# A gated two-layer network with attention and experts on one core: biases of the second attention, order of its statistics, fillers of the search, and scatters of list halves

## Chip, cores and metric

The kernel runs on one core of one Trainium2 chip. The metric is the time of one launch on the device, in microseconds (us). Before the change it is 1257.83 us, the median of three runs (1257.43 to 1258.2).

The engines are named as in the profile: PE is TensorE (PEld its weight loads), DVE is VectorE, ACT is ScalarE, POOL is GpSimd, SP is SyncE, which here only issues DMAs.

## What is computed

`x` holds 8 batches of 256 tokens with 256 features, `ctx` the same shape. Everything is float32. Two layers follow each other, each of an attention and a feed-forward part with experts:

```python
x = x + tanh(g_xattn[0]) * attention0(layernorm(x), ctx, ctx)     # 16 heads of 16, causal mask
x = x + tanh(g_ffn[0])   * ffn0(layernorm(x))                     # 8 experts, each token goes to 2
x = x + tanh(g_xattn[1]) * attention1(layernorm(x), ctx, mask)    # 16 heads of 16, mask on keys
x = x + tanh(g_ffn[1])   * ffn1(layernorm(x))                     # 16 experts + a shared one
```

In `ffn1` it is the experts who choose: a softmax over 16 experts gives scores, and each expert takes the 256 tokens with the highest score (of 2048):

```python
scores = softmax(flat_x @ gate_w.T).T               # 16 x 2048
topk_weight, topk_idx = top_k(scores, 256)
h  = gelu(flat_x[topk_idx] @ Wg[e].T) * (flat_x[topk_idx] @ Wu[e].T)
eo = (h @ Wd[e].T) * topk_weight[..., None]
out = zeros.at[topk_idx].add(eo) + (gelu(x @ Sg.T) * (x @ Su.T)) @ Sd.T     # the last term: the shared expert
```

## The kernel before

A scheduler orders the instructions of DVE, ACT, POOL and SP. PE's order is that of the program text wherever the text stands in `manual_schedule`, and every engine works through its instructions in order. All 2048 tokens lie in SBUF as 16 tiles of 128 tokens (`x`); a batch is two tiles.

**Stages.** First attention (about 0 to 340 us), the routing of the first FFN (337 to 358), its 8 experts (358 to 538, 22.45 us each), then the remaining projections of keys and values for the second attention (`Kv1`, 538 to 551.9), the second attention (551.9 to about 813), the choice of tokens for the 16 experts (813 to 897), the 16 experts (897 to 1247, 22.24 us each) and the last scatter (to 1258.5).

**First FFN** (`ffn0`, L745). An expert transposes its gathered rows (`rtr`, L765), multiplies (`b` L775, `a` L777, `yps` L785) and adds its results to the rows of a table in memory through a scatter of GpSimd (`Router.add`, L646; the four scatters of one expert do not wait for each other, but for those of the expert before). At its end it finds the tokens of the expert after the next (`find_tokens`, a one-hot matrix `hot` and a product `idp`).

**Second attention** (`attention1`, L805). Its first lines load weights and biases and work out, for every batch, whether any key is valid (`some`), the query's bias (`bqs`) and the output's bias with the values' bias folded in (`gb`, for which PE multiplies `bv_wide` by `wo` into `gb_ps`, L847). Then come 32 units, `u = 4 b + ch`: batch `b`, and four heads `ch`. For each unit `find_maxima` multiplies queries and keys (`sc`, L901) and takes the maximum for each query (`maxima`, L906, four instructions on DVE); `weigh` multiplies again with the maximum folded in (`scT`, L933) and takes the exponential on ACT (`pT`, L940); `values_of` multiplies by the values (`o_ps`, L949). Every second unit `place_maxima` transposes the maxima (`mtr`, L922) and adds them to the queries (`qT`, L924); `normalise` divides (`on` L962, `o` L970), `put_back` transposes (`otr`, L982), and once a batch `project_out` multiplies by `wo` (`y`, L990) and adds to `x` (L994). `Net.attend` (L137) writes down in which order PE takes these.

Inside `find_maxima` the next batch is prepared: with `ch == 0` the statistics of its layer norm (`norm_stats`, L88), with `ch == 1` its normalisation and transposition (`norm_pair`, L112: `xn` on DVE, L116, and `ln_ps` on PE, L121), with `ch` 2 and 3 the two halves of its query projection (`qproj`, L877; bias and mask on DVE, L889, and ACT, L885). `norm_stats` is 16 instructions for a batch: two `bn_stats` (L94), two `bn_aggr` (L95) and twelve on 128 x 2 elements (L100 to L107) that take a reciprocal square root, each working on the result of the one before. Once a batch is done with attention, `Last.stats` and `Last.norm` do the same for the last layer norm (`xn3`), and `Last.score` its router's softmax.

**Choice of tokens** (`Last.choose`, L1142). The 256th highest score of each expert is found by a search over 30 bits: on DVE a count (`hit`, L1175), on PE its sum (`total`, L1183), on DVE the decision (`drop` L1185, `cand` L1190), and the next bit. So that PE has work meanwhile, the shared expert is a Python generator (`share`, L1099) of 96 steps, and `fill(n)` puts its next `n` steps into PE's order. A step is two records of 128 x 512 or four of 128 x 256 in the trace. It is called with `1 + bit % 2` in each bit (L1195), and with 2, 2, 4 and the rest around the list making: `prefix` (L154) numbers the chosen tokens, DVE turns this into `marks` and `q16`, and `find_tokens(e)` (L1245) makes `hot` (L1252), `idp` (L1258) and `ids` (L1264), with which GpSimd gathers the rows (L1269).

**Experts** (`Last.experts`, L1274). An expert takes 256 tokens as two halves of 128 (`rtr` L1297, `g` and `u` L1310, `act` L1315, `hT` L1316, `ey` L1320, `eo` L1325); each half is added to `out` by a scatter of GpSimd (L1328). The scheduler sees two scatters that read and write `out`, and so lets each wait for the one before.

Of the kernel before, what the change touches and what calls it, by code (L numbers as in the profile page):

```python
# [41 lines left out]
class Net:  # L42
# [92 lines left out]
    def attend(self, n, find_maxima, place_maxima, weigh, values_of, normalise, put_back, extra):  # L135

        with self.tc.manual_schedule(engines={mybir.EngineType.PE}):  # L137
            for s in range(n + 6):
                g = (s - 2) // 2
                if s < n:  # L140
                    find_maxima(s)
                if 0 <= s - 4 < n:
                    values_of(s - 4)
                if s % 2 == 0 and 0 <= g < n // 2:
                    place_maxima(g)
                if s % 2 == 1 and 0 <= g - 2 < n // 2:
                    put_back(g - 2)
                if 0 <= s - 3 < n:
                    weigh(s - 3)
                if s % 2 == 0 and 0 <= g - 2 < n // 2:  # L150
                    normalise(g - 2)
                extra(s)

    def prefix(self, psum, mask, n, tag="a", last=True):  # L154
# [288 lines left out]
class Router:  # L443
# [54 lines left out]
    def take_x(self):  # L498
        for b in range(B):
            t = slice(2 * b, 2 * b + 2)  # L500
            self.after_puts(self.net.nc.sync.dma_start(self.net.x[:, t, :], self.sum_rows[:, t, :]))

    def after_puts(self, dma):
        for name in self.puts:
            self.net.tc.add_manual_dep(
                dma.ins, name,
                mybir.DependencyInfo(mybir.DependencyClass.Sync, mybir.DependencyReason.DATA),
            )

# [136 lines left out]
    def add(self, e, ids, ys):  # L646


        tc = self.net.tc
        done = []  # L650
        for i, y in enumerate(ys):
# [4 lines left out]
            )  # L656
            group = f"sums{e}"
            tc.declare_no_dep(put.ins, group=group, reason="other rows")
            tc.add_to_no_dep_group(group, put.ins)
            self.after_puts(put)  # L660
            done.append(put.ins.name)
# [82 lines left out]

def ffn0(net, w, router, work, nexts, kv1):  # L745

    tc, nc = net.tc, net.nc
    with ExitStack() as es:
# [4 lines left out]
        for e in range(E0):  # L753
# [48 lines left out]
def attention1(net, w, tanh_g, kT, v, router, last, ps_s):  # L802

# [5 lines left out]
    with ExitStack() as es:  # L809
# [6 lines left out]
        wq = one.tile([P, 2, 4, P], F32, name="wq1")  # L816
        wo = one.tile([P, 2, D], F32, name="wo1")
        bq = one.tile([P, 4], F32, name="bq1")
        gb = one.tile([P, D], F32, name="gb1")
        nc.sync.dma_start(wq, w["wq1"])  # L820
        nc.sync.dma_start(bq, w["bq1"])
        nc.sync.dma_start(wo, w["wo1"])
        nc.sync.dma_start(gb, w["bo1"].partition_broadcast(P))

        mask8 = one.tile([P, N], U8, name="mask8b")
        row16 = one.tile([P, 1], F32, name="row16")
        nc.sync.dma_start(mask8, w["mask"].rearrange("a b -> (a b)").partition_broadcast(P))
        nc.sync.dma_start(row16, w["row16"])
        some = one.tile([P, B], F32, name="some")
        rows = one.tile([P, B], F32, name="some_rows")  # L830
        bqs = one.tile([P, B, 4], F32, name="bqs")
        nc.vector.tensor_reduce(some, mask8.rearrange("p (b k) -> p b k", b=B), AX.X, ALU.min)
        nc.vector.tensor_scalar(some, some, -1.0, 1.0, ALU.mult, ALU.add)
        nc.vector.tensor_scalar(rows, some, row16, None, ALU.max)
        nc.vector.tensor_tensor(
            bqs, bq.unsqueeze(1).to_broadcast([P, B, 4]),
            rows.unsqueeze(2).to_broadcast([P, B, 4]), ALU.mult,
        )

        bv = one.tile([P, 2], F32, name="bv1")  # L840
        wide = one.tile([P, 2, P], F32, name="bv1_wide")
        nc.sync.dma_start(bv, w["bv1"])
        nc.vector.tensor_copy(wide, bv.unsqueeze(2).to_broadcast([P, 2, P]))
        ps = ps_s.tile([P, D], F32, name="gb_ps", tag="s")
        with tc.manual_schedule(engines={mybir.EngineType.PE}):
            for kc in range(2):
                nc.tensor.matmul(ps, wide[:, kc, :], wo[:, kc, :], start=kc == 0, stop=kc == 1)  # L847
        nc.vector.tensor_tensor(gb, gb, ps, ALU.add)
        nc.vector.tensor_scalar(gb, gb, tanh_g, None, ALU.mult)

# [42 lines left out]
        def find_maxima(u):  # L893
# [11 lines left out]
            for r in range(4):  # L905
                nc.vector.tensor_reduce(  # L906
                    m[:, u % 2, :, 32 * r + HD + 1], sc[r], AX.X, ALU.max, negate=True
                )
# [119 lines left out]
class Last:  # L1028
# [3 lines left out]
    def __init__(self, net, w, dram, one, few, xnT, tanh_g, out):  # L1032
# [24 lines left out]
        self.shared = None  # L1057

    def stats(self, b):
        self.st = self.net.norm_stats(self.few, (2 * b, 2 * b + 1), 2)  # L1060
# [38 lines left out]
    def share(self, psum):  # L1099
# [3 lines left out]
        for blk in range(N // 512):  # L1103
# [16 lines left out]
            for i in range(4):  # L1120
                t = 4 * blk + i
                y = psum.tile([P, D], F32, name="sy", tag="s")
                for f in range(FS // P):
# [4 lines left out]
                    if f == 3:  # L1128
# [3 lines left out]
                        )  # L1132
                        nc.sync.dma_start(out[:, t, :], o)
                    if f % 2:
# [6 lines left out]
    def choose(self, one, psum):  # L1141

        self.list = one
        with self.net.tc.manual_schedule(engines={mybir.EngineType.PE}):
            self.find_places(one, psum)
            self.fill(2)
            self.nexts = [self.find_tokens(0, psum, "s")]
            self.fill(4)
            self.nexts.append(self.find_tokens(1, psum, "s"))
            self.fill(96)  # L1150

    def find_places(self, one, psum):
# [27 lines left out]
        for bit in range(29, -1, -1):  # L1180
# [39 lines left out]
        )  # L1220
        self.fill(2)
        nc.vector.scalar_tensor_tensor(
# [52 lines left out]
    def experts(self):  # L1275
        net, w, out = self.net, self.w, self.out
        tc, nc = net.tc, net.nc
        with ExitStack() as es:
# [7 lines left out]
            for e in range(E1):  # L1286
# [16 lines left out]
                for f2 in range(F1 // P // 2):  # L1303
# [11 lines left out]
                    nc.scalar.activation(act, g, AF.Gelu)  # L1315
                    nc.vector.tensor_tensor(hT[:, 2 * f2 : 2 * f2 + 2, :], act, u, ALU.mult)  # L1316
                for r in range(2):
                    y = ps_y.tile([P, D], F32, name="ey", tag="y")
                    for f in range(F1 // P):
# [7 lines left out]
                    )  # L1327
                    nc.gpsimd.indirect_dma_start(  # L1328
                        out=out[:, :],
                        out_offset=bass.IndirectOffsetOnAxis(ap=ids[:, r : r + 1], axis=0),  # L1330
                        in_=o, in_offset=None, compute_op=ALU.add,
                    )
                if e + 2 < E1:
                    self.nexts.append(self.find_tokens(e + 2, ps_a, "a"))
# [3 lines left out]
def network(ctx, tc, w, out):  # L1338
# [11 lines left out]
    with ExitStack() as right, ExitStack() as left:  # L1350
# [11 lines left out]
        with ExitStack() as psum:  # L1362
            ps_s = pool(psum, "a0_ps_s", 7, space=PSUM)
            kv1 = Kv1(net, ctxT, w, k1, v1, ctxs, ps_s)
            attention0(net, ctxT, w, tanh_g[:, 0, 0:1], router, kept, ps_s, kv1)
            one, work = pool(left, "f0_one"), pool(left, "f0_work", 2)
            nexts = router.place(one, work, kv1, ps_s)
        ffn0(net, w, router, work, nexts, kv1)
    one, few = pool(ctx, "f1_one", side="right"), pool(ctx, "f1_few", 2, side="right")
    last = Last(net, w, dram, one, few, k1[0], tanh_g[:, 1, 1:2], out)  # L1370
    with ExitStack() as psum:
        ps_s = pool(psum, "a1_ps_s", 7, space=PSUM)
        attention1(net, w, tanh_g[:, 0, 1:2], k1, v1, router, last, ps_s)
        values.close()
# [85 lines left out]
```

## Time and profile before

| what | value |
|---|---|
| median of three runs | 1257.83 us (1257.43 to 1258.2) |
| the profiled execution | 1260.25 us, span 1258.5 us |
| mean granted TensorE clock | 0.979 |
| PE busy | 1198.6 us, 95% of the span |
| PEld / DVE / ACT / POOL busy | 846.0 / 581.9 / 320.9 / 268.7 us |
| PE idle, second attention's first 48 us | 8.1 us, clock 0.75 there |
| PE idle, search (813 to 861) | 2.8 us |
| PE idle, list making (861 to 897) | 4.9 us, clock 0.95 there |

PE is the engine that sets the time, and a busy share of 95% leaves 59.9 us idle in all. The granted clock says more than the busy time does: the same instruction takes twice as long at 0.5, and is counted as busy for all of it. Of the timeline's columns the first is the start in us, the second the time from the first to the last instruction of a group, then engine, line, operation, the tiles (out<-in), shape and how many; in brackets stands the engine's idle time before it and what ended it. Records that follow closely are put into one row, so a row can hold short idle times.

### The profile page before, as it was taken

To read this page: it belongs to the slowest core of one execution; us is meant where nothing else is said; L and a number is where in the kernel's file an instruction comes from. 1 tells how busy PE (TensorE), PEld (TensorE's weight loads), DVE (VectorE), ACT (ScalarE), POOL (GpSimd) and SP (SyncE) were. 2 spreads that over 40 slices of the span, in tenths; PEclk is the share of its full clock that TensorE was granted. 3 is DMA by queue.
4 is the path that set the end of the run, shared out by engine and by line. 5 is a ranking of instruction groups with operands and counts; after the bars stand their busy time and mean duration, and the time that the engine had idled before them with its cause. 6 is when DMAs were issued, how large, how long until landed. Compare 5 with 4: busy or idle time off the path is not lost.

```text
span 1258.5 us, 21894 instructions
## 1 busy us (share of the span) xinstructions
PE 1198.6 (95%) x9145; PEld 846.0 (67%) x9145; DVE 581.9 (46%) x1485; ACT 320.9 (25%) x629; POOL 268.7 (21%) x329
## 2 busy tenths in 40 slices
PE   5899999999999999988999999998999999999997
PEld 5556667777546565555666665644788888888886
DVE  5634656554524332267766675567332232322221
ACT  2333344344221111122444445210101111110110
POOL 1200222232036455230000000000122232322211
PEclk9899999999999999987999999999999999999999
DMA  7000101001425456140000000420165554646531
GB/s 232 2 2 11 60 2 35 18 19 35 137 65 118 106 125 155 27 134 1 1 6 14 11 10 10 161 100 17 54 196 148 184 167 151 191 131 189 165 109 17
DMA packets 49665, 104.31 MB, mean 83 GB/s; under 512 B 7834, under 2 KB 35742, under 8 KB 43294
## 3 DMA queue, kind: packets, MB, share of 16 engines
q1 hardware_dynamic: 37278, 85.73, 19.8%
q0 software_dynamic: 12288, 17.18, 8.2%
q8 instruction: 72, 1.18, 0.4%
q14 instruction: 27, 0.22, 0.0%
HBM read 85.39 MB, written 17.50 MB: 82 GB/s over the span
## 4 chain that ended last, share of the span: by engine, by line
PE 89%; DVE 6%; ACT 1%; DMA 1%; issue 1%; SPq 0%; POOLq 0%; POOL 0%; DVEq 0%; ACTq 0%
PE g L1310 9%; PE u L1310 9%; PE ey L1320 9%; PE proj L237 6%; PE b L775 5%; PE yps L785 4%; PE a L777 4%; PE sc L901 3%; PE scT L933 3%; PE o_ps L949 3%; PE sc L297 3%; PE o_ps L349 2%; PE qproj L877 2%; PE y L394 2%; PE scT L329 2%; PE su_ps L1110 2%
## 5 line engine op out<-in xcount | busy, mean ns | idle before, releaser
L1310 PE MATMUL g<-rT,ge 128*128 128x256 f32 x512 | 121.6, 380 | 5.0 <-issue 4.8
L1316 DVE TENSOR_TENSOR hT<-act,u 128x512 f32<-128x512 f32 x64 | 44.0, 688 | 166.6 <-PE u L1310 159.1
L1310 PE MATMUL u<-rT,ue 128*128 128x256 f32 x512 | 120.9, 379 | 0.0
L1328 POOL DMA_INDIRECT out<-eo,ids x32 | 62.6, 1958 | 255.7 <-DVE eo L1325 206.1
L1320 PE MATMUL ey<-de,hT 128*128 128x256 f32 x512 | 113.1, 379 | 0.0
L1310 PEld LDWEIGHTS g<-rT,ge 128*128 128x128 f32 x512 | 96.1, 190 | 18.1 <-issue 5.2
L1310 PEld LDWEIGHTS u<-rT,ue 128*128 128x128 f32 x512 | 97.3, 190 | 13.2
L1320 PEld LDWEIGHTS ey<-de,hT 128*128 128x128 f32 x512 | 97.3, 190 | 13.2
L1315 ACT ACTIVATE act<-g 128x512 f32<-128x512 f32 x64 | 38.2, 597 | 243.4 <-PE g L1310 241.2
L906 DVE TENSOR_REDUCE maxima<-sc 128x2 f32<-128x512 f32 x128 | 79.4, 684 | 26.2 <-PE sc L901 26.2
L337 POOL TENSOR_SCALAR_AFFINE_SELECT pT<-pT 128x256 f32<-128x256 f32 x128 | 50.4, 414 | 156.1 <-ACT pT L336 156.1
L307 DVE TENSOR_REDUCE maxima<-sc 128x3 f32<-128x384 f32 x128 | 62.4, 552 | 34.0 <-PE sc L302 34.0
L652 POOL DMA_INDIRECT xsum<-y,to x32 | 56.9, 1779 | 93.2 <-DVE y L790 85.9
L940 ACT ACTIVATE pT<-scT 128x512 f32<-128x512 f32 x128 | 66.1, 602 | 36.9 <-PE scT L933 36.9
L901 PE MATMUL sc<-kept,qT 32*128 32x256 f32 x512 | 60.4, 424 | 5.8 <-ACT pT L940 3.0
L775 PE MATMUL b<-rT,ve 128*128 128x512 f32 x128 | 63.1, 611 | 0.5 <-ACT rT L76 0.5
L780 DVE TENSOR_TENSOR hT<-a,sb 128x512 f32<-128x512 f32 x32 | 22.1, 692 | 85.3 <-PE a L777 79.9
L336 ACT ACTIVATE pT<-scT 128x384 f32<-128x384 f32 x128 | 52.4, 496 | 34.6 <-PE scT L329 34.6
L777 PE MATMUL a<-rT,we 128*128 128x512 f32 x128 | 61.1, 595 | 0.0
L1325 DVE TENSOR_SCALAR eo<-ey,rows,tanh_g 128x256 f32<-128x256 f32 x32 | 17.4, 544 | 89.7 <-PE ey L1320 89.7
L785 PE MATMUL yps<-oe,hT 128*128 128x256 f32 x256 | 56.6, 379 | 0.0
L785 PEld LDWEIGHTS yps<-oe,hT 128*128 128x128 f32 x256 | 48.6, 190 | 10.0 <-issue 3.8
(253 smaller groups left out, 1868.2 us busy)
## 6 DMA issues: line engine op xcount, KB each, us to landing
ge<-g SPq DMA_DIRECT2D x16, 1024.0 KB, 4.8
ue<-u SPq DMA_DIRECT2D x16, 1024.0 KB, 6.3
de<-d SPq DMA_DIRECT2D x16, 1024.0 KB, 4.8
we<-w SPq DMA_DIRECT2D x8, 512.0 KB, 4.2
ve<-v SPq DMA_DIRECT2D x8, 512.0 KB, 3.6
oe<-o SPq DMA_DIRECT2D x8, 512.0 KB, 5.6
table<-xn SPq DMA_DIRECT2D x8, 272.0 KB, 2.2
ctxT<-ctxT SPq DMA_DIRECT2D x4, 512.0 KB
```

The source lines that it names most:

```text
L237: nc.tensor.matmul(ps[32 * j : 32 * j + 32, :], wt[:, kc, c, :], src[:, kc, b * S : (b + 1) * S], start=kc == 0, stop=kc == 1,)
L307: nc.vector.tensor_reduce(m[:, u % 2, :, 32 * j + HD + 1], sc[j], AX.X, ALU.max, negate=True)
L652: put = self.net.nc.gpsimd.indirect_dma_start(out=self.sums[:, :], out_offset=bass.IndirectOffsetOnAxis(ap=ids[:, i : i + 1], axis=0), in_ ...
L775: nc.tensor.matmul(b, ve[:, kc, cols], rT[:, kc, :], start=kc == 0, stop=kc == 1)
L777: nc.tensor.matmul(a, we[:, kc, cols], rT[:, kc, :], start=kc == 0, stop=kc == 1)
L785: product = nc.tensor.matmul(ps, hT[:, f, r * P : (r + 1) * P], oe[:, f, :], start=f == 0, stop=f == F0 // P - 1,)
L901: nc.tensor.matmul(sc[r][:, qt, :], q[rows, ch, qt * P : (qt + 1) * P], k[rows, :], start=True, stop=True,)
L906: nc.vector.tensor_reduce(m[:, u % 2, :, 32 * r + HD + 1], sc[r], AX.X, ALU.max, negate=True)
L940: nc.scalar.activation(p, sc[r], AF.Exp, scale=SCALE)
L1310: nc.tensor.matmul(dst[:, i, :], wt[:, kc, f * P : (f + 1) * P], rT[:, kc, :], start=kc == 0, stop=kc == 1,)
L1320: nc.tensor.matmul(y, hT[:, f, r * P : (r + 1) * P], de[:, f, :], start=f == 0, stop=f == F1 // P - 1,)
L1328: nc.gpsimd.indirect_dma_start(out=out[:, :], out_offset=bass.IndirectOffsetOnAxis(ap=ids[:, r : r + 1], axis=0), in_=o, in_offset=None, c ...
```

## The change

Four edits, none of which changes what is computed.

1. The lines of `attention1` that work out `wo`, `gb`, `some` and `bqs` become a function `biases1`. `ffn0` calls it after its expert 1 has issued its scatters and found the tokens of expert 3. Its tiles come from a pool of their own, its psum tile from the FFN's pool. The load of `wq` stays in `attention1`.
2. In `find_maxima` the statistics of the next batch may only be issued after the fourth maximum of the unit with `ch == 0`. Until now the scheduler was free to issue them any time after their `x` was loaded.
3. Each bit of the search gets two steps of the shared expert (before: one or two in turn); the calls around the list become 3, 3, 2 in place of 2, 2, 4.
4. The two scatters of an expert no longer wait for each other, but for the scatters of the expert before (those of the first expert for the shared expert's writes). The helper serves `Router.add` and `take_x` too, where the dependences stay as they were.

In the order of the instructions, edit 1 puts the six loads on SP and the DVE operations for `some`, `bqs` and `bv_wide` into the end of the first attention, and the `gb_ps` product to the boundary between the FFN's experts 1 and 2. With edit 2, DVE's order in batches 4 to 7 is: output sum, `Last`'s statistics, its `xn`, four maxima, the attention's statistics with the `qT` sum among them, the attention's `xn`, `den`, `o`, four maxima. PE's order in the attention stays.

```diff
+    def unordered(self, put, group, puts):
+        self.tc.declare_no_dep(put.ins, group=group, reason="other rows")
+        self.tc.add_to_no_dep_group(group, put.ins)
+        self.wait_for(put, puts)
+
+    def wait_for(self, dma, puts):
+        for name in puts:
+            self.tc.add_manual_dep(
+                dma.ins, name,
+                mybir.DependencyInfo(mybir.DependencyClass.Sync, mybir.DependencyReason.DATA),
+            )
...
@@ ffn0
             if e + 2 < E0:
                 nexts.append(router.find_tokens(e + 2, ps_a, "a"))
+            if e == 1:
+                meanwhile(ps_a, "a")
...
+def biases1(net, w, tanh_g, one, psum, tag):
...
+    ps = psum.tile([P, D], F32, name="gb_ps", tag=tag)
+    for kc in range(2):
+        nc.tensor.matmul(ps, wide[:, kc, :], wo[:, kc, :], start=kc == 0, stop=kc == 1)
+    nc.vector.tensor_tensor(gb, gb, ps, ALU.add)
+    nc.vector.tensor_scalar(gb, gb, tanh_g, None, ALU.mult)
+    return wo, gb, some, bqs
...
@@ find_maxima
             for r in range(4):
-                nc.vector.tensor_reduce(
+                last_max = nc.vector.tensor_reduce(
                     m[:, u % 2, :, 32 * r + HD + 1], sc[r], AX.X, ALU.max, negate=True
                 )
             if b + 1 < B:
                 if ch == 0:
-                    stats[b + 1] = net.norm_stats(work, (2 * b + 2, 2 * b + 3), 2)
+                    with tc.issue_after(last_max.ins):
+                        stats[b + 1] = net.norm_stats(work, (2 * b + 2, 2 * b + 3), 2)
...
@@ choose
             self.find_places(one, psum)
+            self.fill(3)
+            self.nexts = [self.find_tokens(0, psum, "s")]
             self.fill(2)
-            self.nexts = [self.find_tokens(0, psum, "s")]
-            self.fill(4)
             self.nexts.append(self.find_tokens(1, psum, "s"))
             self.fill(96)
...
@@ find_places
-            self.fill(1 + bit % 2)
+            self.fill(2)
...
-        self.fill(2)
+        self.fill(3)
...
@@ experts
+                done = []
                 for r in range(2):
...
-                    nc.gpsimd.indirect_dma_start(
+                    put = nc.gpsimd.indirect_dma_start(
                         out=out[:, :],
...
+                    net.unordered(put, f"out{e}", self.puts)
+                    done.append(put.ins.name)
+                self.puts = done
```

More of the change, by code (lines that the diff above doesn't have):

```diff
@@ L500, in take_x @@
             t = slice(2 * b, 2 * b + 2)
[L501 to L508, printed above, removed]
+            load = self.net.nc.sync.dma_start(self.net.x[:, t, :], self.sum_rows[:, t, :])
+            self.net.wait_for(load, self.puts)
     def norm(self, stats, i, pair, pool, psum, tag):
@@ L646, in add @@
     def add(self, e, ids, ys):
-        tc = self.net.tc
         done = []
@@ L656, in add @@
             )
[L657 to L660, printed above, removed]
+            self.net.unordered(put, f"sums{e}", self.puts)
             done.append(put.ins.name)
@@ L742, in values, with ffn0 @@
         )
-def ffn0(net, w, router, work, nexts, kv1):
+def ffn0(net, w, router, work, nexts, kv1, meanwhile):
     tc, nc = net.tc, net.nc
@@ L799, in ffn0, with attention1 @@
             kv1.fill(64)
-def attention1(net, w, tanh_g, kT, v, router, last, ps_s):
+def biases1(net, w, tanh_g, one, psum, tag):
+    nc = net.nc
+    wo = one.tile([P, 2, D], F32, name="wo1")
+    bq = one.tile([P, 4], F32, name="bq1")
+    gb = one.tile([P, D], F32, name="gb1")
+    nc.sync.dma_start(bq, w["bq1"])
+    nc.sync.dma_start(wo, w["wo1"])
+    nc.sync.dma_start(gb, w["bo1"].partition_broadcast(P))
+    mask8 = one.tile([P, N], U8, name="mask8b")
+    row16 = one.tile([P, 1], F32, name="row16")
+    nc.sync.dma_start(mask8, w["mask"].rearrange("a b -> (a b)").partition_broadcast(P))
+    nc.sync.dma_start(row16, w["row16"])
+    some = one.tile([P, B], F32, name="some")
+    rows = one.tile([P, B], F32, name="some_rows")
+    bqs = one.tile([P, B, 4], F32, name="bqs")
+    nc.vector.tensor_reduce(some, mask8.rearrange("p (b k) -> p b k", b=B), AX.X, ALU.min)
+    nc.vector.tensor_scalar(some, some, -1.0, 1.0, ALU.mult, ALU.add)
+    nc.vector.tensor_scalar(rows, some, row16, None, ALU.max)
+    nc.vector.tensor_tensor(
+        bqs, bq.unsqueeze(1).to_broadcast([P, B, 4]),
+        rows.unsqueeze(2).to_broadcast([P, B, 4]), ALU.mult,
+    )
+    bv = one.tile([P, 2], F32, name="bv1")
+    wide = one.tile([P, 2, P], F32, name="bv1_wide")
+    nc.sync.dma_start(bv, w["bv1"])
+    nc.vector.tensor_copy(wide, bv.unsqueeze(2).to_broadcast([P, 2, P]))
+    ps = psum.tile([P, D], F32, name="gb_ps", tag=tag)
[4 more added lines that the diff above has]
+    return wo, gb, some, bqs
+def attention1(net, w, tanh_g, kT, v, biases, router, last, ps_s):
     tc, nc, x = net.tc, net.nc, net.x
@@ L816, in attention1 @@
         wq = one.tile([P, 2, 4, P], F32, name="wq1")
-        wo = one.tile([P, 2, D], F32, name="wo1")
-        bq = one.tile([P, 4], F32, name="bq1")
-        gb = one.tile([P, D], F32, name="gb1")
         nc.sync.dma_start(wq, w["wq1"])
[L821 to L849, printed above, removed]
+        wo, gb, some, bqs = biases
         maxima = [one.tile([P, 2, 2, P], F32, name=f"maxima{i}") for i in range(2)]
@@ L1057, in __init__ @@
         self.shared = None
+        self.puts = []
     def stats(self, b):
@@ L1132, in share @@
                         )
-                        nc.sync.dma_start(out[:, t, :], o)
+                        put = nc.sync.dma_start(out[:, t, :], o)
+                        self.puts.append(put.ins.name)
                     if f % 2:
@@ L1365, in network @@
             attention0(net, ctxT, w, tanh_g[:, 0, 0:1], router, kept, ps_s, kv1)
+            before1 = pool(values, "a1_biases")
             one, work = pool(left, "f0_one"), pool(left, "f0_work", 2)
             nexts = router.place(one, work, kv1, ps_s)
-        ffn0(net, w, router, work, nexts, kv1)
+        biases = []
+        ffn0(
+            net, w, router, work, nexts, kv1,
+            lambda *ps: biases.extend(biases1(net, w, tanh_g[:, 0, 1:2], before1, *ps)),
+        )
     one, few = pool(ctx, "f1_one", side="right"), pool(ctx, "f1_few", 2, side="right")
@@ L1372, in network @@
         ps_s = pool(psum, "a1_ps_s", 7, space=PSUM)
-        attention1(net, w, tanh_g[:, 0, 1:2], k1, v1, router, last, ps_s)
+        attention1(net, w, tanh_g[:, 0, 1:2], k1, v1, biases, router, last, ps_s)
         values.close()
```

## The prediction

> **What bounds the kernel now.** I read the chain that ended last first:
>
> ```profile
> PE 89%; DVE 6%; ACT 1%; DMA 1%; issue 1%; SPq 0%; POOLq 0%; POOL 0%; DVEq 0%; ACTq 0%
> ```
>
> TensorE carries nearly everything, so an edit is worth what it does to TensorE's idle time, its clock, or its order. Where TensorE loses time is told by the windows by stage (length, then busy time with records for PE, PEld, DVE, ACT, POOL; then granted clock):
>
> ```profile
> 551.90:600.00 48.10, 40.01 (x248) 26.17 (x248) 37.09 (x133) 12.10 (x23) 7.54 (x10) 0.75 0.13 45
> 600.00:792.50 192.50, 189.38 (x1747) 122.28 (x1746) 128.58 (x348) 90.80 (x194) 5.80 (x12) 1.00 0.05 16
> 813.00:861.00 48.00, 45.18 (x151) 22.85 (x150) 31.93 (x135) 6.06 (x9) 0.00 (x0) 1.00 0.27 95
> 861.00:897.00 36.00, 31.13 (x153) 19.50 (x153) 21.18 (x36) 2.83 (x6) 3.92 (x4) 0.95 0.13 42
> ```
>
> The head of the second attention (first row) is the only stage with a low clock, 0.75; the rest of that attention, the search and the list are nearly full. TensorE's waits name the releasers (total, times, longest):
>
> ```profile
> PE idp L1258 <- DVE hot L1252: 4.5, 1, 4.5
> PE ln_ps L121 <- DVE xn L116: 3.1, 1, 3.1
> PE sc L901 <- ACT pT L940: 3.0, 9, 0.7
> PE total L1183 <- DVE hit L1175: 2.5, 5, 0.7
> PE sc L901 <- DVE maxima L906: 2.4, 2, 1.4
> ```
>
> And windows of 3.41 us, placed where the granted clock steps:
>
> ```profile
> 553.79:557.20 3.41, 0.66 (x4) 0.40 (x4) 3.41 (x25) 0.00 (x0) 0.63 (x1) 1.00 0.91 368
> 557.20:560.61 3.41, 2.73 (x7) 2.19 (x7) 3.41 (x14) 0.59 (x1) 2.40 (x4) 0.50 0.63 229
> ...
> 581.09:584.50 3.41, 3.20 (x21) 1.73 (x20) 3.17 (x7) 0.14 (x1) 0.00 (x0) 1.00 0.00 0
> 584.51:587.92 3.41, 2.36 (x12) 1.36 (x12) 0.00 (x0) 3.38 (x6) 0.00 (x0) 0.50 0.00 0
> ```
>
> A window with little work is followed by half clock. It was at half from 557.2 to 564.0, 570.9 to 577.7 and 584.5 to 594.7.
>
> **Biases earlier: cost +1.8, gain within the head.** Two `gb_ps` matmuls (four records, 1.13 us at 552.33) now stand at a boundary of the first FFN, where TensorE has no gap, and shift the rotation of the psum banks there, so that the second half of `rtr` waits for the copy of the first: +1.6 (1.1 to 2.0). The vector operations of the masks (about 4 us in all, at 307 to 313) go before the router's choice, where VectorE has 5.55 us idle until 319.4: +0.2 (0 to 0.3). Their six DMA issues, 0.38 to 0.48 us each by the rows of the `x` loads, enter SP's queue ahead of the last `xtab` put, some 30 us before the gathers: hidden. The eight `x` loads (543.4 to 554.2) now follow one another and land no later.
>
> **Head: -8.8.** Today VectorE, in program order, runs bias work and statistics of several batches before the first `xn` (556.07); TensorE stands 3.08 us, and `qproj` takes 6.70 us at half clock where 16 records at 0.216 make 3.46. Counted from the last K/V matmul (551.88): changed, `ln_ps` needs only the copy it waits for now (0.46), its own 0.58, ACT's copy with issue 0.86, so `qproj` runs from +1.9 to +5.35, full clock (now +12.8). Then `qT` 0.55 and four maxima of 0.60 end at +8.5. Now the new order costs: batch 1's statistics stand behind these maxima and among the next four: 0.67 + 0.33 + 2.4 + 12 x 0.195 + half an `xn` 0.33 make +14.5 for `ln_ps` (now +17.2). TensorE idles from +7 to +14.5, so I charge about 5 us of half clock after it. Scores, `qproj`, `mtr`, scores, `qproj` bring the first `scT` to its end at +25.7 (now about +31.8), the 1.28 us table load and `pT` to +28.9 (now 588.30, +36.4), and `o_ps`, `mtr`, `scT`, `sc`, 5.2 at full and 6.7 at partly half clock, to batch 2's `ln_ps` at +34.1 to +35.6, where 595.70 is +43.8. Gain 8.2 to 9.7; I take 8.8. Ends: -5 if the half clock stays three windows, as from 584.5, and -11 with none.
>
> **Steady batches: +11.1, and clock +2.0.** This is the price of the same edit. Now, VectorE and then TensorE in a batch:
>
> ```profile
> 640.70 0.74 DVE L116 TENSOR_SCALAR xn<-x,ln_mv,ln_r 128x256 f32<-128x256 f32 x2
> 641.35 2.48 DVE L906 TENSOR_REDUCE maxima<-sc 128x2 f32<-128x512 f32 x4
> 643.75 0.68 DVE L924 TENSOR_TENSOR qT<-qT,mtr 128x512 f32<-128x512 f32 x1
> ```
>
> ```profile
> 645.69 0.66 PE L121 MATMUL ln_ps<-ident,xn 128*128 128x128 f32 x4
> 646.28 1.07 PE L949 MATMUL o_ps<-pT,kept 128*32 128x256 f32 x16
> ```
>
> The `xn` at 640.70 has its statistics ready long before, and `ln_ps` waits for nothing. Changed, the router's `xn` takes that slot, so the maxima still end at 643.75; behind them stand two BN statistics 0.67, an aggregate 0.17, the `qT` sum 0.69, an aggregate 0.17, twelve steps of 0.195 and half an `xn`: 0.67 + 0.17 + 0.69 + 0.17 + 2.34 + 0.33 gives 648.1. `ln_ps` waits 2.5 us, and all of TensorE's queue stands behind it: `o_ps`, `otr`, the next `scT`; ACT and VectorE follow these, so nothing is won back later in the 27.47 us of a batch. Four batches (4 to 7) pay 2.5; batch 3, with no output chain ahead, 1.1: 11.1 (8 to 12.5). Will a 2.5 us gap halve the clock? 1.9 us idle at 867.8 to 871.2 did not, 2.6 us at 871.2 to 874.6 did; with the windows' unknown phase I count two of four, each 1.7 lost less 0.7 of a stall at 649.31 that it swallows: 2.0. Ends: 0, and 9.6 for four times two windows.
>
> The Trainium skill, "TensorE: Matmul & The Clock Gate", Part 1 (the HAM clock gate), has the clock halved after one idle window of about 3.4 us. By that rule these gaps would cost no clock, and the sum below would be 2.0 lower. The row of 581.09 speaks against it: 3.20 us are shown busy there, and half clock followed; the measurement decides.
>
> **Search: -4.8.** A step is 0.86 us. A one-step bit now takes 1.17 (844.42 to 845.59), a two-step bit 1.82 (845.59 to 847.41): the second step costs 0.65, so 15 more save 15 x 0.21 = 3.2 of later time. Fifteen pairs make 45, the stage 47.8: the 2.8 beyond are `shT` and `so` operations within the chain of a one-step bit; in two-step bits the chain with them (1.84) is about TensorE's time, so 1.6 of the 2.8 go. Ends: -3.2, -6.
>
> **List: -2.5.** Of the 4.49 us before `idp`, two more steps fill 1.7; VectorE's own chain is 0.2 shorter. But only six steps instead of 19 and more then cover the gathers. `hot` 1 stands ahead of the first `ids`: from the prefix, `idp` +7.75, `ids` +10.9, gathers issued from +11.2 and +12.5, landing 2.4 to 3.4 later by the DMA activity after 879.19; the fillers end at +14.9, the first expert's matmuls start at about +18. Without its 12 steps (10.3) that is 7.7; now 31.9 less 25 steps (21.5) is 10.4. So -2.7, taken 2.5; ends -3.5, and +2 if a gather takes the 4.0 us of the first FFN's.
>
> **Scatter: -1.4.** At the very end:
>
> ```profile
> 1247.98 3.82 DMA out<-eo,ids
> 1251.80 0.02 issue
> 1251.83 0.02 POOLq L1328
> 1251.84 0.79 issue
> ```
>
> The second half's `eo` is done at 1251.15 and its scatter issues at 1252.86; free, it issues 0.27 after, at 1251.42. Between experts POOL is off the path. Ends: 0, -1.5.
>
> **Sum:** 1.6 + 0.2 - 8.8 + 11.1 + 2.0 - 4.8 - 2.5 - 1.4 = -2.6. The profiled execution took 1260.25 (span 1258.5 and 1.75 around), 2.42 above the median of 1257.83; the sum applies to either: 1255.2.
>
> **Rivals.** (1) The clock: every 2.5 us gap costs two half windows, 2.4 each: +9.6 for 2.0, so 1262.8, slower. It decides from about two such drops on. For it: three drops in the head, with gaps of 1 us. Against: steady windows never fell. (2) The wait doesn't appear in full, because TensorE's other stalls (0.7 at 649.31, 1.2 in the `scT` of 641.48) shrink as VectorE catches up: 1.2 a batch, no clock: 1255.2 - 5.2 - 2.0 = 1248. Against: they come from the same queues, shifted alike. (3) The gathers are bare: +2 for -2.5, and one half window, 1.7: 1261.4.
>
> **Chances.** Forecast 0.42 (own range 1251 to 1259.5: faster 0.23, same 0.15, slower 0.04); clock 0.25 (same 0.02, slower 0.23); absorbed 0.20 (faster); gathers 0.13 (faster 0.02, same 0.04, slower 0.07). Together faster 0.45, same 0.21, slower 0.34, where 0.2%, 2.5 us, is about what a measurement can tell. The range, 1247 to 1265, takes in the rivals' times.
>
> **What would show it.** Right: `ln_ps` waiting for `xn` about 2.5 us four times between 600 and 800; `qproj` at full clock first; batch 2's `ln_ps` some 9 us earlier after K/V; totals 1.82 to 1.88 apart; two last scatters 3.5 apart. Wrong: no such waits, half clock between 600 and 800, or `rtr` waiting over 3 us for `rows`.

## The result

The changed kernel takes 1266.41 us, the median of eight runs (1260.92 to 1269.45), beside 1258.21 us for the kernel before, measured with it (1257.43 to 1260.15): a ratio of 1.0059, 95% interval 1.0042 to 1.0075. It is slower, by 0.6%. Forecast were 1255.2 us, faster, with a range of 1247 to 1265. Of the rivals, the first (the clock, 1262.8) and the third (the gathers, 1261.4) had the right sign, and both fell short.

The changed kernel's runs lie 8.5 us apart, those of the kernel before 2.7. That is taken up below, and is not settled.

The profiled execution of the changed kernel took 1266.44 us, span 1264.2, which is 5.7 over the span before. The medians differ by 8.2. Of the 2.5 us between the two, 2.0 come from the execution profiled before, which with 1260.25 us was slower than all eight runs; 0.5 lie outside the spans. Between marks on TensorE the two executions differ like this (us; a step of the shared expert is charged with its 0.86):

| stretch | before | after | difference | forecast |
|---|---|---|---|---|
| start to the end of the last K/V matmul | 551.9 | 553.7 | +1.8 | +1.8 |
| head: from there to batch 2's `ln_ps` | 43.8 | 35.2 | -8.6 | -8.8 |
| steady batches: from there to the first `ln_ps` behind batch 4's `y` (758.1, 767.4) | 162.4 | 178.5 | **+16.1** | +13.1 |
| from there to the first `total` | 55.8 | 55.8 | 0 | 0 |
| search, to the end of `prefix`, less 15 steps (12.9) | 52.0 | 59.2 | -5.7 | -4.8 |
| list, to the first `g`, plus 15 steps | 31.9 | 21.2 | **+2.2** | -2.5 |
| experts and end | 360.7 | 360.6 | -0.1 | -1.4 |

The chain that ended last, of the changed kernel: TensorE's share has gone from 89% to 85%, VectorE's from 6% to 8%.

```profile
PE 85%; DVE 8%; DMA 2%; issue 2%; ACT 1%; SPq 1%; POOL 0%; POOLq 0%; ACTq 0%; DVEq 0%
```

The windows by stage of the changed kernel (head, steady batches, search, list; columns as before: length, busy time of PE, PEld, DVE, ACT, POOL, then the granted clock):

```profile
553.70:602.00 48.30, 38.39 (x314) 25.98 (x315) 30.95 (x80) 15.48 (x29) 3.02 (x4) 0.89 0.10 35
602.00:795.00 193.00, 180.66 (x1644) 114.04 (x1642) 129.05 (x380) 84.05 (x181) 8.63 (x15) 0.97 0.03 9
823.00:877.00 54.00, 54.00 (x186) 29.91 (x185) 32.98 (x136) 7.25 (x11) 0.00 (x0) 1.00 0.26 93
877.00:904.00 27.00, 19.44 (x124) 12.33 (x123) 19.97 (x35) 2.04 (x4) 7.14 (x4) 0.98 0.13 40
```

The head's clock rose from 0.75 to 0.89, and it does 314 matmul records in its 48 us where it did 248. The search has no idle time left (54.00 of 54.00). But the steady batches, once 189.4 us busy of 192.5, are now 180.7 of 193.0, and their clock is no longer 1.00. The list is busy for 19.4 us of 27. TensorE's longest waits for other engines, from 536 to 900 us:

```profile
PE ln_ps L121 <- DVE xn L116: 15.6, 7, 6.3
PE sc L912 <- ACT pT L952: 3.4, 9, 1.2
PE idp L1273 <- DVE hot L1267: 2.1, 2, 1.5
PE rtr L1312 <- DMA rows<-table,ids: 2.1, 1, 2.1
PE sy L1138 <- DVE shT L1132: 1.0, 1, 1.0
```

Just behind 900 us `rtr` waits a second time for `rows`, so that these two waits make 4.2 us, over the 3 us that the prediction names as a sign of being wrong. `ln_ps` waits seven times: 6.3 us once in the head, 0.8 and 1.1 for batches 2 and 3, and about 1.9 for each of batches 4 to 7. For batch 6 that looks like this, first VectorE, then TensorE (start, time, what; in brackets the idle time before and its releaser):

```profile
701.50 0.74 DVE L94 BATCH_NORM_STATS2 ln_st<-x 128x6 f32<-128x256 f32 x2
702.16 0.17 DVE L95 BATCH_NORM_AGGREGATE ln_mv<-ln_st 128x2 f32<-128x6 f32 x1
702.24 0.66 DVE L936 TENSOR_TENSOR qT<-qT,mtr 128x512 f32<-128x512 f32 x1
...
705.40 0.74 DVE L116 TENSOR_SCALAR xn<-x,ln_mv,ln_r 128x256 f32<-128x256 f32 x2
```

```profile
702.95 1.14 PE L912 MATMUL sc<-kept,qT 32*128 32x256 f32 x14 [0.17 <-DVE qT L936]
705.96 0.67 PE L121 MATMUL ln_ps<-ident,xn 128*128 128x128 f32 x4 [1.86 <-DVE xn L116]
706.56 1.07 PE L961 MATMUL o_ps<-pT,kept 128*32 128x256 f32 x16
```

From the end of the maxima at 701.5 to `xn` at 705.4 VectorE works without a gap on chains of small instructions, and TensorE stands for 1.86 us with everything else behind it. From the end of the maxima to `ln_ps` it is 4.46 us, where the kernel before has 1.95 in this batch: 2.5 more. Of these, 1.86 are the wait shown, and 0.64 are lost in the `sc` ahead of it, whose `qT` sum now stands behind the batch statistics (the 0.17 above, and idle time within the row of the first two `sc`). A batch takes 30.2 us instead of 27.5: these 2.5, and 0.27 because VectorE's next maxima are late too: the row of `scT` after `ln_ps` takes 0.67 us longer, and the next `sc` wins 0.40 of it back.

Then the clock. In the profile it steps between full and half on a grid of 3.41 us. These are the windows of that grid around the waits of batches 4, 6 and 7:

```profile
640.06:643.47 3.41, 1.55 (x22) 0.92 (x20) 2.99 (x15) 0.07 (x2) 0.78 (x1) 1.00 0.00 0
643.47:646.88 3.41, 3.41 (x30) 1.71 (x33) 2.48 (x5) 1.33 (x3) 0.74 (x2) 0.50 0.00 0
...
701.49:704.91 3.42, 2.43 (x21) 1.42 (x20) 3.07 (x16) 1.83 (x4) 0.00 (x0) 1.00 0.00 0
704.91:708.32 3.41, 2.37 (x27) 1.39 (x28) 3.27 (x10) 1.21 (x3) 1.52 (x2) 1.00 0.00 0
...
732.22:735.63 3.41, 1.94 (x18) 1.00 (x16) 2.96 (x16) 1.33 (x3) 0.00 (x0) 1.00 0.00 0
735.63:739.04 3.41, 2.85 (x20) 1.31 (x20) 3.37 (x8) 0.58 (x1) 1.51 (x2) 0.50 0.00 0
```

All these waits are 1.9 us long. All of batch 4's and most of batch 7's fall into one window, where TensorE is busy for 1.55 and 1.94 us, and the next window is at half; so it is with batch 5's (1.76 us, half clock from 674.2 to 677.6). Batch 6's is shared by two windows, with 2.43 and 2.37 us of work, and the clock stays full. Among these four, then, it goes by the place of the wait on the grid. A rule by busy share alone it is not: in the list 1.43 us of work from 896.06 to 899.47 were followed by full clock, and in the prediction's row of 581.09 3.20 us by half. In e2's execution (below) the drops came with batches 5, 6 and 7, from 671.5, 705.7 and 736.4 us on, and none with batch 4.

The end went as forecast. The second `eo` begins at 1257.76, and its scatter goes out at once, 3.45 us after the first:

```profile
1255.13 1.55 POOL L1344 DMA_INDIRECT out<-eo,ids  x1 [15.71 <-DVE eo L1341]
1257.76 0.54 DVE L1341 TENSOR_SCALAR eo<-ey,rows,tanh_g 128x256 f32<-128x256 f32 x1 [2.91 <-PE ey L1336]
1258.58 1.55 POOL L1344 DMA_INDIRECT out<-eo,ids  x1 [1.90 <-DVE eo L1341]
```

### The profile page after: what moved, and what is told of

Its sections match the earlier page's. It is cut to its first block, busy times and chain, and to the rows that moved or that the text cites. A ratio compares the mean times of both kernels' runs of the same rounds, so it can differ in the third digit from the quotient of the medians.

```text
span 1264.2 us, 21883 instructions
## 1 busy us (share of the span) xinstructions
PE 1193.4 (94%) x9145; PEld 838.6 (66%) x9145; DVE 579.7 (46%) x1485; ACT 320.8 (25%) x629; POOL 260.0 (21%) x329
## 4 chain that ended last, share of the span: by engine, by line
PE 85%; DVE 8%; DMA 2%; issue 2%; ACT 1%; SPq 1%; POOL 0%; POOLq 0%; ACTq 0%; DVEq 0%
PE g L1325 9%; PE u L1325 9%; PE ey L1336 8%; PE proj L250 6%; PE b L778 5%; PE a L780 4%; PE yps L788 4%; PE o_ps L961 3%; PE sc L912 3%; PE sc L310 3%; PE y L407 2%; PE scT L945 2%; PE qproj L888 2%; PE o_ps L362 2%; PE scT L342 2%; PE kproj L725 2%
## 5 line engine op out<-in xcount | busy, mean ns | idle before, releaser
L1344 POOL DMA_INDIRECT out<-eo,ids x32 | 50.9, 1592 | 251.2 <-DVE eo L1341 251.2
L917 DVE TENSOR_REDUCE maxima<-sc 128x2 f32<-128x512 f32 x128 | 79.5, 682 | 30.3 <-PE sc L912 30.2
L1284 POOL DMA_INDIRECT rows<-table,ids x32 | 34.9, 1091 | 101.7 <-DVE idf L1278 72.9
```

The source lines that it names most:

```text
L917: last_max = nc.vector.tensor_reduce(m[:, u % 2, :, 32 * r + HD + 1], sc[r], AX.X, ALU.max, negate=True)
```

## The experiments

**The theory (W)**: the second edit's statistics, ahead of `ln_ps` in VectorE's order, make TensorE wait in every batch, and these waits cost clock. **The rival (L)**: the loss comes from the moved biases and from the list. All kernels are compared by their ratio to the kernel before, measured beside them on the same chip; its medians there lie between 1258.2 and 1259.9 us. A ratio's interval is 1 to 3 us wide to either side, so differences of 2 or 3 us between two kernels are read with care.

| kernel | median | ratio to before, 95% interval |
|---|---|---|
| changed kernel | 1266.41 | 1.0059 (1.0042 to 1.0075) |
| e1: without the second edit | 1251.78 | 0.9933 (0.9920 to 0.9947) |
| e2: second edit alone | 1271.34 | 1.0095 (1.0081 to 1.0109) |
| e3: third edit alone | 1256.72 | 0.9981 (0.9972 to 0.9990) |
| e4: first edit alone | 1254.98 | 0.9959 (0.9945 to 0.9973) |
| e5: changed kernel, waits of batches 4 to 7 filled with matmuls | 1263.77 | 1.0034 (1.0023 to 1.0044) |
| e6: as e7, `hot` after the gathers | 1247.92 | 0.9905 (0.9891 to 0.9919) |
| e7: statistics half a batch earlier | 1250.08 | 0.9931 (0.9918 to 0.9944) |
| e8: as e7, other steps in the last ten bits | 1247.65 | 0.9911 (0.9897 to 0.9926) |
| e9: fourth edit alone | 1257.29 | 0.9991 (0.9982 to 1.0000) |
| e10: e6, e8 and e11 together | 1243.46 | 0.9881 (0.9863 to 0.9899) |
| e11: as e7, batch 1's statistics free | 1240.42 | 0.9860 (0.9836 to 0.9883) |
| e12: e6 and e11 together | 1242.04 | 0.9860 (0.9843 to 0.9876) |

### The four edits one by one: e1 to e4, e9

e1 takes the second edit out of the changed kernel:

```diff
-                    with tc.issue_after(last_max.ins):
-                        stats[b + 1] = net.norm_stats(work, (2 * b + 2, 2 * b + 3), 2)
+                    stats[b + 1] = net.norm_stats(work, (2 * b + 2, 2 * b + 3), 2)
```

> The changed kernel with its second edit undone: the scheduler may issue the statistics of the next batches early again. Theory W (the statistics behind the maxima make TensorE wait in every batch, and these waits halve the clock for a window at times): the four waits of 1.9 us before ln_ps between 600 and 770 go, batches are 27.5 us again, no half clock there, and the stage from batch 2 to the end of the attention is 16 us shorter; of the 8.6 us won at the head some 3 to 5 are lost again. In all 11 to 13 us below the changed kernel, so about 1254. Rival L (the loss comes from the moved biases and from the list): the kernel stays at 1262 or above.

It is faster than the kernel before, and 16 us faster than the changed one (1.0059 less 0.9933 of 1258), where 11 to 13 were expected. From 590 to 770 us `ln_ps` doesn't appear among TensorE's waits any more, the clock is 1.00, and the stretch from batch 2 on takes 162.3 us again (178.5). The head takes 37.2 us: without the second edit 1.9 of its 8.6 us are lost, less than the 3 to 5 expected. Theory W holds; L falls, as the account of the whole loss.

e2 puts the same lines alone into the kernel before.

> The kernel before with the second edit alone. Theory W: steady batches 30.2 us, some with half clock after the wait, +16 us from batch 2 on; the head wins 3 to 5 us against before. About 1269 to 1271, slower than the changed kernel. Rival L: about 1258, like before.

11.9 us slower, the upper end of W's range. TensorE's waits from 590 to 770 us:

```profile
PE ln_ps L121 <- DVE xn L116: 8.5, 5, 1.9
PE sc L901 <- ACT pT L941: 2.0, 7, 0.3
PE sc L901 <- DVE qT L925: 0.7, 4, 0.2
```

The five waits of batches 3 to 7 are there without any other edit, the head is 5.7 us shorter (38.1 for 43.8), and the stretch from batch 2 on takes 179.7 us.

e3 changes only the four calls of `fill`.

> The kernel before with the third edit alone (two steps a bit; 3, 3, 2 around the list). Theory W: the search wins 5 to 6 us; the list, whose gathers now stand bare and behind the hot operation of VectorE, costs 2 against my forecast of a gain; in all -2 to -4, so 1254.5 to 1256. Rival L: the bare gathers cost more than the search wins, 1260 or above.

2.4 us faster: what W expected at its lower end. Search and `prefix` take the same 59.2 us as in the changed kernel, the list 21.1, so the same +2.1. Here three of the four gathers are slow on GpSimd:

```profile
884.97 1.06 POOL L1269 DMA_INDIRECT rows<-table,ids  x1 [72.86 <-DVE ids L1264]
886.34 2.42 POOL L1269 DMA_INDIRECT rows<-table,ids  x1 [0.32 <-issue]
889.07 2.34 POOL L1269 DMA_INDIRECT rows<-table,ids  x1 [0.31 <-issue]
891.72 3.04 POOL L1269 DMA_INDIRECT rows<-table,ids  x1 [0.30 <-issue]
```

e4 keeps only the first edit, `biases1` within the FFN (in code, the changed kernel with the lines of the other three as they were).

> The kernel before with the first edit alone. Theory W: +1.8 until the end of the first FFN, and -4 to -7 in the head, whose first projection then runs at full clock: 1253 to 1256. Rival L: the moved biases cost more than they win, 1260 or above.

5.2 us faster. Its head takes 37.8 us. So of the head's 8.6 us either of the two edits alone brings 5.7 to 6.1: the gains overlap. Over all kernels here, the last K/V matmul ends at 552.9 us on average with the moved biases (ten executions, 551.7 to 554.0) and at 550.9 without (four, 549.8 to 551.9): the move costs about 2.0, as forecast, though not where: on average 1.6 by the `prefix` of the first router, near 338 us (forecast 0.2), and 0.4 from there on (forecast 1.6). Single executions differ by up to 5 us at that mark, so the split is rough. What the traces show of the places: in the changed kernel's first attention `otr` waits 1.0 us for VectorE, which has the biases' `some` (2.29 us) ahead of `osb`; in the FFN the boundary between the experts 1 and 2 is 1.3 us longer, within the forecast range, but the FFN's start wins most of this back.

e9 gives the kernel before only the unordered scatters.

> The kernel before with the fourth edit alone. My forecast for it was -1.4 us, all of it at the very end: the second half's last scatter issues 0.27 us after its eo instead of 1.7. Theory: 1256.5 or so, ratio 0.9985 to 0.9995, the last two scatters 3.5 us apart instead of 4.9, nothing moved before. Rival (scatters side by side disturb each other or the weights' loads): no faster, or slower.

1.1 us faster, at the edge of what the interval tells from no change; the stretch from the last matmul to the end is 6.5 us for 7.9 in its trace, so the forecast's 1.4 holds.

### Do the waits cost clock? e5

Four matmuls without use (eight records) go ahead of `ln_ps` in batches 4 to 7, into the bank that `ln_ps` then overwrites:

```diff
+        if warm is not None:
+            for _ in range(4):
+                self.nc.tensor.matmul(
+                    ps[:, 0], warm[:, 0, 0, :], warm[:, 1, 0:2, :], start=True, stop=True
+                )
...
-                ps_s, "s", xnTs[b], nc.scalar.copy,
+                ps_s, "s", xnTs[b], nc.scalar.copy, warm=wq if b > 3 else None,
```

> The changed kernel with eight records of matmul without use (1.73 us) ahead of ln_ps in batches 4 to 7, where TensorE waits 1.9 us; they write into the bank that ln_ps overwrites. Theory W: the three windows at half clock between 640 and 740 don't come, batches stay at 30.2 us, and the kernel is 3 to 5 us faster than the changed one, with less spread. Rival (the half clock has nothing to do with these waits): no faster.

3.1 us faster than the changed kernel by the ratios, with more work in it. 100 us of the steady batches, in the changed kernel and then in e5:

```profile
640.00:740.00 100.00, 90.98 (x803) 57.87 (x803) 70.88 (x217) 39.12 (x85) 6.69 (x11) 0.95 0.03 10
```

```profile
640.00:740.00 100.00, 98.27 (x861) 64.44 (x860) 71.59 (x221) 41.78 (x91) 6.71 (x11) 1.00 0.03 10
```

No half clock is left, and batches take 30.3 us each, so the stretch from batch 2 on falls from 178.5 to 175.1. Of the 16.1 us lost there, 3.4 are clock, a little over 1.1 for each of the three drops, and 12.7 are waits. The runs lie 5.7 us apart (1259.95 to 1265.64), less than the changed kernel's 8.5 but still more than the 2.7 of the kernel before. The clock also drops elsewhere (at 888 and 898 us here), so the spread isn't explained by these waits alone.

### Is it the place in the order? e7 and e11

In e7 the statistics of batches 1 and 2 stay where the change puts them, all later ones come half a batch earlier:

```diff
+            if ch == 2 and 0 < b < B - 2:
+                with tc.issue_after(last_max.ins):
+                    stats[b + 2] = net.norm_stats(work, (2 * b + 4, 2 * b + 5), 2)
             if b + 1 < B:
-                if ch == 0:
+                if ch == 0 and b < 2:
                     with tc.issue_after(last_max.ins):
                         stats[b + 1] = net.norm_stats(work, (2 * b + 2, 2 * b + 3), 2)
...
```

> The changed kernel, but from batch 1 on the statistics are issued half a batch earlier: those of batch b + 2 behind the maxima of unit ch == 2 of batch b, where VectorE has idle time. Theory W (the price of the second edit is only its place ahead of ln_ps in VectorE's order): no wait of ln_ps for xn in batches 4 to 7, batches of 27.5 us, no half clock there, and the head as short as in the changed kernel (35 us from the K/V projections to batch 2's ln_ps): some 2 us below the kernel with the second edit undone, 16 below the changed one. Rival (any statistics in the steady batches delay the maxima, and what is won at the head is lost again): not below the kernel with the second edit undone, ratio to before 0.993 or more.

The same 16 instructions, placed where VectorE has time, cost next to nothing: 0.3 us of the 16.1. From 590 to 760 us:

```profile
590.00:760.00 170.00, 167.97 (x1595) 110.76 (x1588) 127.78 (x365) 79.93 (x170) 8.62 (x15) 1.00 0.03 8
```

No wait of `ln_ps`, clock 1.00, 162.6 us for the stretch. The head takes 35.6 us, 1.6 less than in e1. The times don't tell e7 from e1 (0.9931 and 0.9933), against the 2 us I expected, so by its number the rival is not excluded; its mechanism is, since the trace shows no delay in the steady batches.

e11 frees batch 1's statistics as well; only batch 2's stay behind their maxima:

```diff
-                if ch == 0 and b < 2:
+                if ch == 0 and b == 0:
+                    stats[1] = net.norm_stats(work, (2, 3), 2)
+                elif ch == 0 and b == 1:
                     with tc.issue_after(last_max.ins):
-                        stats[b + 1] = net.norm_stats(work, (2 * b + 2, 2 * b + 3), 2)
+                        stats[2] = net.norm_stats(work, (4, 5), 2)
```

> As the kernel with the statistics half a batch earlier, but batch 1's statistics may be issued as soon as their x is there; those of batch 2 stay behind their maxima. There TensorE waits 6.3 us for batch 1's xn in one piece and runs some 11 us at half clock after it. Theory: the statistics were right to wait only where VectorE is late; ahead of the first maxima it is idle, so the wait of 6.3 us shrinks to 1 or 2, with less half clock, and the stretch from the K/V projections to batch 2's ln_ps falls from 35.5 to 29 to 31 us: 4 to 6 us faster. Rival (that wait covers other work that is then late: qT, maxima, the exponential's table load): less than 2 us faster.

8.9 us faster than e7, more than expected. The head in the changed kernel, and then in e11:

```profile
559.10 3.04 PE L912 MATMUL sc<-kept,qT 32*128 32x256 f32 x32
568.43 1.09 PE L121 MATMUL ln_ps<-ident,xn 128*128 128x128 f32 x4 [6.29 <-DVE xn L116]
```

```profile
559.16 3.04 PE L912 MATMUL sc<-kept,qT 32*128 32x256 f32 x32
562.13 0.66 PE L121 MATMUL ln_ps<-ident,xn 128*128 128x128 f32 x4
562.71 2.47 PE L912 MATMUL sc<-kept,qT 32*128 32x256 f32 x16
```

The wait of 6.29 us is gone, `ln_ps` runs at full clock, and the head takes 29.2 us: 6.4 less than in e7. The rest of the 8.9 lies in the list (19.1 us for 21.5), where in this execution the first three gathers happened to begin ahead of a `hot` or clear of it (0.94 to 1.06 us; the fourth took 1.89). e11 is, with e12, the fastest version of the study, 1.4% below the kernel before.

### The list: e6, e8, e10, e12

In the changed kernel the list lost where I had forecast a gain. Its gathers on GpSimd, then VectorE beside them:

```profile
894.27 2.99 POOL L1284 DMA_INDIRECT rows<-table,ids  x1 [72.87 <-DVE idf L1278]
897.57 2.26 POOL L1284 DMA_INDIRECT rows<-table,ids  x1 [0.30 <-issue]
900.13 0.95 POOL L1284 DMA_INDIRECT rows<-table,ids  x1 [0.30 <-issue]
```

```profile
894.05 2.28 DVE L1267 TENSOR_TENSOR hot<-cols,q 128x2048 bf16<-128x2048 bf16 x1
...
896.72 2.28 DVE L1267 TENSOR_TENSOR hot<-cols,q 128x2048 bf16<-128x2048 bf16 x1
```

The first gather begins 0.22 us after a `hot` and ends 0.93 after that `hot` ends; the second ends 0.83 after the next `hot`. The third, with no `hot` beside it, takes 0.95. e6 holds the `hot` of the experts 2 and 3 back until GpSimd has issued the four gathers, through a small write of GpSimd behind them:

```diff
-        nc.vector.tensor_tensor(
+        mark = nc.vector.tensor_tensor(
...
+        if e in (2, 3):
+            net.wait_for(mark, [self.issued])
...
-            nc.gpsimd.indirect_dma_start(
+            gather = nc.gpsimd.indirect_dma_start(
...
+        if e == 1:
+            flag = few.tile([P, 1], F32, name="flag")
+            with net.tc.issue_after(gather.ins):
+                self.issued = nc.gpsimd.memset(flag, 0.0).ins.name
```

> As the kernel with the statistics half a batch earlier, but the hot operations of experts 2 and 3 on VectorE wait until GpSimd has issued the four gathers of experts 0 and 1. In the changed kernel the first two of these took 2.99 and 2.26 us on GpSimd, the next two 0.95, and hot ran beside the first two. Theory P (GpSimd's issue of a gather stands still while this operation of VectorE runs, if that came first): all four take about 1.0 us, and rtr waits less than 1 us for rows; since hot of expert 2 is later by about as much, the time changes by less than 1.5 us. Rival (the first gathers after a long pause are slow, or wait for the table): the first two still take over 2 us.

```profile
877.98 1.06 POOL L1289 DMA_INDIRECT rows<-table,ids  x1 [72.86 <-PE idp L1278]
879.34 0.96 POOL L1289 DMA_INDIRECT rows<-table,ids  x1 [0.31 <-issue]
880.61 0.95 POOL L1289 DMA_INDIRECT rows<-table,ids  x1 [0.30 <-issue]
```

All four take 0.94 to 1.06 us, the first of them after 72.86 us of pause, so theory P holds and the rival falls: the gathers stood still behind `hot`. (In e7, without this edit, three of the four take 2.55 to 3.03.) `rtr`'s waits for rows are gone, and `idp` waits 2.7 us for `hot` instead. The list takes 19.6 us, 1.9 less than in e7. The time is 3.3 us less than e7's by the ratios and 2.2 by the medians, where I had allowed 1.5; with four and five runs that is not clearly more.

e8 leaves `hot` alone and covers the gathers with five steps from the search:

```diff
-            self.fill(2)
+            self.fill(2 if bit >= 10 else 1 + bit % 2)
```

> As the kernel with the statistics half a batch earlier, but the last ten bits of the search get one or two steps in turn, so that five more steps of the shared expert (4.3 us) stand between the second list and the first expert. Theory of the bare gathers: rtr's waits for rows, 4.2 us in two, fall below 0.5, while the ten bits lose about 1.5 us again: 2 to 3 us faster than without. Rival (the gathers' place costs nothing, because the list's own chain on VectorE ends as late): no gain, 1 to 2 us slower.

2.5 us faster than e7 by the ratios, as expected, and `rtr` no longer waits for `rows`; but the parts are others than expected. Apart from the five steps the list is 3.0 us shorter and the search 2.6 longer, not 1.5, so the two nearly cancel. Of the 2.1 us between the two spans, 1.4 lie in the experts: e7 has a window of half clock in the first one (886.6 to 890.1), e8 none. That the number came out as expected was in part luck.

> Statistics half a batch earlier, batch 1's free, the last ten bits with one or two steps, and hot of experts 2 and 3 after the gathers. If the gains add: 4 to 6 below the kernel with the last two of these, which alone gave 2 to 2.5 each; both serve the same gathers, so together hardly more than one: about 1242, ratio to before 0.986 to 0.988.

e10 comes out at the upper edge of what was expected, 0.9881. By the ratios it is 2.6 us slower than e11, which has neither cure, but the intervals overlap. In the traces the list takes 24.4 us with five more steps (4.3 us), 20.1 without them (e11: 19.1), and the search loses 2.6 us for these steps: both cures serve the same gathers, and their prices remain.

> Statistics half a batch earlier, batch 1's free, and hot of experts 2 and 3 after the four gathers; two steps in every bit. Of the two cures for the bare gathers this is the one that takes no step from the search. Theory P: the four gathers are issued in 1.0 us each in every execution, the list takes 19.5 us (21.5 without the cure in the kernel that it was measured against), so 1 to 2 us below the kernel with batch 1's statistics free, about 1239. Rival (that kernel's gathers came first by luck of its order already, so there is nothing left to win): within 1 us of it.

e12 has the same ratio as e11, 0.9860. The list takes 19.7 us with `hot` held back, 19.1 in e11's execution, where the gathers came first without help. So far as intervals of 2 us either way can tell, the rival was right: nothing to win on top of e11.

## Why the prediction was wrong

Between the two traces the change is +5.7 us where -2.6 was forecast, 8.3 more. Of these the list has 4.7, the steady batches 3.0 and the experts 1.3; the head adds 0.2, and the search takes 0.9 off. The list's miss by itself turns the sign, and the steady batches' adds to it.

1. **"Steady batches: +11.1, and clock +2.0": the right mechanism, sized too small.** The cost appeared in the forecast place and was 16.1 us: 12.7 of waits (e5) and 3.4 of clock. The sum of VectorE's chain was right: `ln_ps` comes 2.5 us later after the maxima, as forecast, though only 1.86 of them show as its wait, because TensorE already lost 0.64 in `sc` behind the `qT` sum. The step that failed is that nothing was charged for what follows `ln_ps`: VectorE's next maxima are late too and hold up `scT`, 0.27 us net in a batch. That makes 1.1 for four batches; another 0.4 is spread over smaller shifts. "Two of four" windows at half were three, each about 1.1, not 1.0. Half clock between 600 and 800 stands in the prediction as a sign of being wrong, although its own sum charged two such windows; so by itself this sign says little.
2. **"List: -2.5" is the step that failed most, by its sign: +2.2.** Two mistakes. There were 27 steps behind the prefix, not 25, so the list before had 8.7 us of other time, not 10.4; that alone makes the forecast -0.8. And the gathers were priced by rows that no `hot` held up (0.95 to 1.06 us): forecast were the two of the first expert issued from +11.2 and +12.5 us after the prefix and the first expert's matmuls at +18; measured were +11.8, +15.1 and +21.2. The rows that I needed stood in the trace of before. There the first FFN's first gather ran into a `hot` and took 2.72 us, the next 0.96:

```profile
348.76 2.72 POOL L636 DMA_INDIRECT rows<-xtab,ids  x1 [11.06 <-DVE idf L642]
351.79 0.96 POOL L636 DMA_INDIRECT rows<-xtab,ids  x1 [0.30 <-issue]
```

```profile
348.16 2.29 DVE L619 TENSOR_TENSOR hot<-cols,q 128x2048 bf16<-128x2048 bf16 x1
```

   Of the skill's pages I had weighed only the one on the clock. The Trainium skill, "SBUF — State Buffer", section "Who interferes with whom", has VectorE and GpSimd share a pair of ports, locked by whichever comes first, and says that a VectorE instruction with two SBUF inputs blocks a GpSimd one that reads SBUF. These rows agree; the page adds an inference that this kind of operation doesn't hold up GpSimd's own DMAs, and with a gather by indices it did (2.99 us in the changed kernel, 0.94 to 1.06 with the operation held back in e6).
3. **Head: -8.8** was right (-8.6), its parts too: `qproj` at full clock took 3.72 us including its last record's end (forecast 3.46), `ln_ps` of batch 1 came 14.8 us after the K/V matmuls (forecast 14.5) after 6.3 us of idle time, batch 2's 35.2 (34.1 to 35.6). But I took the whole for the price of keeping the order; e1 and e4 show that the first edit alone brings 6, and e11 that the order itself still cost 6.4 us there.
4. **Biases: +1.8** was right in sum (2.0 on average), wrong in its parts (on average 1.6 and 0.4 for 0.2 and 1.6): the operations that I laid into VectorE's idle time at 319 stood ahead of `osb`, for which `otr` waited 1.0. The boundary in the FFN cost 1.3 of the forecast 1.6, but most of it was won back there; that the sum came out right was luck.
5. **Search: -4.8** was -5.7: nearly all of the stalls went, not 1.6 of 2.8. **Scatter: -1.4** was right.
6. **The experts** carried 1.3 us that I had not listed: half clock at 902.9 to 906.3, in the first expert, after `rtr`'s waits. The third rival had this half window.
7. **The range** reached 1265 because it took the rivals one at a time. Two came together, clock and waits +3.0 and list +4.7, and the experts' 1.3 with them.

Not settled: how much of the runs' wide spread comes from these drops of the clock. e5, without them, still spreads over 5.7 us, e11, without the waits in the steady batches, over 8.6, and only one execution of each kernel was traced in detail.

## What to carry to other kernels

Putting work "behind" something frees an engine where it was late, and costs where its result is the next thing waited for: for each place, add up the engine's queue from the last instruction that must go first to the one that the bound engine waits for, and move only the instances that gain (here batch 2's statistics; batch 1's belong earlier, the others half a batch earlier, in all -1.4% in place of +0.6%). When filler work is taken from behind a transfer, look in the trace for a row of that transfer with the neighbours that it will have now, not for its shortest row. Edits that gain by the same idle time don't add up: here two with 6 us each made 8.6 together.

## What was not expected of the hardware

- The issue of a gather by indices on GpSimd stands still while a VectorE `TENSOR_TENSOR` of 128 x 2048 bf16 runs, if that began first: 1.89 (e11) to 3.15 us (e1) in place of 0.94 to 1.06, ending 0.8 to 1.0 us after it. In the trace of before, a gather that began 0.02 us ahead of a `hot` (at 880.56) took 0.96. That `hot` was not held up in turn: it took 2.30 us, for 2.28 otherwise.
- A wait of TensorE of 1.9 us was followed by half clock in the next window in three cases of four in the changed kernel, where its window of 3.41 us held 1.55 to 1.94 us of work; the fourth, shared by two windows with 2.43 and 2.37 us of work, cost no clock. A drop in the steady batches cost about 1.1 us.
